# The order of a neighbourhood's 126 pixels on the partitions of an involution kernel: row by row instead of column by column

## The chip, the cores and the metric

The kernel runs on one core of a Trainium2 chip. The metric is the device time of that core in microseconds, from the start of the program to its end. One launch does the whole computation; the host only lays out weights.

## The reference, cut to what matters

The input is a batch of 8 images with 256 channels of 56 x 56 pixels in float32. Two blocks follow each other, each added to its own input.

```python
# block 0: an involution, whose 7 x 7 filter differs at every pixel, on the group-normalised input
ker = einsum('bchw,oc->bohw', gn(x), w_reduce) + b_reduce        # 256 -> 64 channels
ker = einsum('bchw,oc->bohw', ker, w_span) + b_span              # 64 -> 16 groups * 49 taps
patches = stack([xpad[:, :, i:i+56, j:j+56] for i in range(7) for j in range(7)])
x = x + (ker * patches).sum(taps)      # 16 channels of a group share a filter
# block 1: two 3 x 3 convolutions with ternary weights, batch norms over the whole batch, relus
out1 = relu(bn(conv(gn(x), tern(w1)))); out2 = bn(conv(out1, tern(w2)))
x = x + relu(out1 + out2)
```

The change touches block 0 alone.

## The kernel before, in words

**Stages.** The involution takes the first 1330 us of the program, image after image. The two convolutions follow, some 430 us of matmuls each, and then a last pass that combines and writes the output. The weights of the convolutions are quantized in the first 190 us.

**How the involution becomes matmuls.** Output pixels are worked on in tiles of PY x PX = 3 x 8. All that such a tile needs lies in a neighbourhood of QY x QX = 9 x 14 = 126 pixels (NQ). These 126 pixels are put on the partitions, which are the contracted dimension of a matmul. One operand is `q`: 126 neighbourhood pixels by 7 tiles (TX, one band across the image) by 128 columns, which are 64 channels in the upper and in the lower half of the image. The other is `a`: for each tile and group, a matrix from 126 neighbourhood pixels to 24 output pixels that holds the filter taps at the right places and zeros elsewhere. `apply_row` (from line 648) multiplies them: 56 small matmuls (line 662) for a band of tiles, whose result is evicted by ScalarE (line 670) and VectorE (line 671) and added to the image by GpSimd (line 674). There are 10 bands (TY), 4 channel quarters (NCQ) and 8 images: 320 bands in all.

**Where `a` comes from.** `generate` (from line 606) multiplies a slice of the stationary `wl` with the reduced features `kr` (line 626), and adds the span bias `bt` while evicting (lines 632 and 638). `wl` is a line of weights with zeros around it. The slice of 126 columns that starts at an offset depending on the output pixel (py, px) puts every tap on the partition of the neighbourhood pixel it belongs to. So the order of the neighbourhood pixels on the partitions enters in three places: in the slice's offset, in the layout of `wl` and `bt` that the host makes, and in the load of `q`.

**Where `q` comes from.** `prep` (from line 538) normalises a quarter of the next image, transposes it on TensorE and stores it with DMAs (line 547) to a scratch tensor in HBM, `xtd`. That tensor has 14 planes, one for each column j of a neighbourhood. A plane holds 36 rows (HQ) of 8 tile places (KX) of 128 floats. Neighbouring planes lie 147,456 B apart, neighbouring rows in a plane 4,096 B. One row of a band, 7 tiles by 128 floats, is contiguous: 3,584 B. `load_q` (line 591) fetches a band with one DMA of 126 such pieces, one for each partition, 441 KB. Before the change the outer dimension of its source is the 14 planes and the inner one 9 rows.

**What sets the order.** The program is written out in one order. In the loop over quarters (line 741) each band runs `apply_row`, then `prefetch`, which issues the load of a later band, up to five in advance (NQB = 5 buffers), then one or two queued transfers (`tasks`: loads of the next image on line 449, stores of finished quarters on line 688, stores to `xtd`), then a tenth of the next quarter's `generate`, then statistics on VectorE. A load's buffer comes free when the matmuls five bands earlier are done. All of these DMAs are issued by SyncE, one after the other. Loads of the next image's pixels are handed out during quarter 0, their statistics run on VectorE in quarter 1, and `prep` runs in quarters 2 and 3. The loads of an image's first bands can be issued only when its stores to `xtd` have been, which happens at the end of quarter 3 (lines 773 to 775).

Of the kernel before, what the change touches and what calls it, by code (L numbers as in the profile page):

```python
# [15 lines left out]
P = 128  # L16
# [3 lines left out]
K, PAD, G = 7, 3, 16  # L20
# [7 lines left out]
NCQ = C // CH  # L28
GQ = G // NCQ
# [4 lines left out]
PY, PX = 3, 8  # L34
TY, TX = 10, W // PX
# [2 lines left out]
NE = 2 * TX  # L38
QY, QX = PY + K - 1, PX + K - 1
NQ = QY * QX  # L40
LEAD = (PX - 1) * QY + PY - 1
WL = LEAD + NQ

KX = TX + 1
HQ = TY * PY + K - 1
EX = HQ * KX
# [26 lines left out]
def involution_tri_block_kernel(  # L75
# [356 lines left out]
    with ExitStack() as ph1:  # L432
# [3 lines left out]
        def ps_tile(name):  # L436
            return ps_p.tile([P, 2, 512], F32, tag="ps", name=name)
# [72 lines left out]
        def reduce(b, py):  # L510

            n = len(range(py, HH, PY))
            for i0 in range(0, n, TY // 2):
                m = min(TY // 2, n - i0)
                ps = ps_tile(f"pk_{b}_{py}_{i0}")
                r0 = i0 * PY + py
                for c in range(NCQ):
                    for h in range(2):
                        rows = slice(h * CH, (h + 1) * CH)
                        src = xs[b, c].rearrange("p (r w) -> p r w", w=W)  # L520
                        nc.tensor.matmul(ps[:, h, :m * W], wrn[rows, c, :],  # L521
                                         src[rows, r0:r0 + (m - 1) * PY + 1:PY, :],
                                         start=(c == 0), stop=(c == NCQ - 1))
                src = ps[:, :, :m * W].rearrange("p h (k x) -> p h x k", x=PX)
                whole = min(m, TY - 1 - i0)
                nc.scalar.activation(
                    kr[py][:, :, :NT].rearrange("p x (h k) -> p h x k", h=2)
                    [:, :, :, i0 * TX:(i0 + whole) * TX],
                    src[:, :, :, :whole * TX], AF.Identity, bias=brn)
                if whole < m:  # L530
                    nc.scalar.activation(
                        kr[py][:, :, NT:].rearrange("p x (h k) -> p h x k", h=2),
                        src[:, :, :, whole * TX:], AF.Identity, bias=brn)
# [57 lines left out]
        def load_q(b, c, ty):  # L591

            q = qpool.tile([P, TX, P], F32, tag="q", name=f"q_{b}_{c}_{ty}")
            d = xt_d[b % 2][c][:]
            src = bass.AP(d.tensor, d.offset + PY * ty * KX * P,
                          [[EX * P, QX], [KX * P, QY], [1, TX * P]])
            nc.sync.dma_start(q[:NQ].rearrange("p k c -> p (k c)"), src)
            return q

        def views(a):  # L600

            n = NT * GQ * NP
            return (a[:NQ, :n].rearrange("q (t f) -> q t f", t=NT),
                    a[:NQ, n:].rearrange("q (t f) -> q t f", t=NE))

        def generate(b, c, a):

            whole, rest = (v.rearrange("q t (g p) -> q g p t", g=GQ) for v in views(a))  # L610
            for u in range(NU):
                gp, (p0, n) = u // len(UNITS), UNITS[u % len(UNITS)]
                ps = ps_tile(f"pg_{b}_{c}_{u}")
                on_act = u in ON_ACT
                nt = NT + (NE if p0 < PX else 0)
                for j in range(n):
                    py, px = (p0 + j) // PX, (p0 + j) % PX
                    o = LEAD - px * QY - py
                    for i in range(2):
                        rows = slice(i * CR, (i + 1) * CR)  # L620

                        if on_act:
                            dst = ps[:NQ, i, j * nt:(j + 1) * nt]
                        else:
                            dst = ps[:NQ, i, j:n * nt:n]
                        nc.tensor.matmul(dst, wl[rows, c, gp, o:o + NQ], kr[py][rows, px, :],  # L626
                                         start=True, stop=True)
                g0 = 2 * gp
                if on_act:
                    for i in range(2):  # L630
                        for j in range(n):
                            nc.scalar.activation(  # L632
                                whole[:, g0 + i, p0 + j], ps[:NQ, i, j * nt:(j + 1) * nt],
                                AF.Identity, bias=bt[:, c, g0 + i, p0 + j:p0 + j + 1])
                else:
                    for dst, t0, t1 in ((whole, 0, NT), (rest, NT, nt)):
                        if t0 < t1:
                            nc.vector.tensor_tensor(  # L638
                                dst[:, g0:g0 + 2, p0:p0 + n].rearrange("q g p t -> q g t p"),
                                ps[:NQ, :, t0 * n:t1 * n].rearrange("q i (t p) -> q i t p", p=n),  # L640
                                bt[:, c, g0:g0 + 2, p0:p0 + n].unsqueeze(2).to_broadcast(
                                    [NQ, 2, t1 - t0, n]),
                                ALU.add)
                if c == NCQ - 1 and b + 1 < B and gp == GP - 1 and p0 + n in (PX, 2 * PX, NP):
                    reduce(b + 1, (p0 + n) // PX - 1)
                yield
# [33 lines left out]
        def prefetch(b):  # L680
            while queue and queue[0][0] <= b and len(loads) < NQB:
                k = queue.pop(0)
                loads[k] = load_q(*k)
# [45 lines left out]
        with tc.tile_pool(name="qp", bufs=1) as qp:  # L729
            quantize(wq_d[0], w1, qp, ps_flat, "w1")  # L730
            for _ in generate(0, 0, a_next):
                pass
            quantize(wq_d[1], w2, qp, ps_flat, "w2")
# [7 lines left out]
        for m, (b, c) in enumerate(quarters):  # L741
            a = a_next
            gen = iter(())
            if m + 1 < len(quarters):
                a_next = matrices(m + 1)
                gen = generate(*quarters[m + 1], a_next)
# [132 lines left out]
```

## Time and profile before

The time is 2488.15 us, the median of 3 runs (2482.87 to 2488.16). The profiled execution has a span of 2489.0 us.

| What | Share or size |
|---|---|
| TensorE matmuls busy, whole span | 1801.8 us, 72% |
| VectorE busy, whole span | 1659.4 us, 67% |
| ScalarE, GpSimd busy | 1093.8 us and 288.1 us |
| mean traffic, whole span | 198 GB/s, 493.14 MB |
| SyncE's DMA queue | 447.66 MB, 56.8% of the 16 DMA engines' span |
| loads of `q` | 320 DMAs of 441.0 KB |
| stores to `xtd` | 64 of 448, 128 of 168, 64 of 48 and 128 of 18 KB |
| loads of x, stores of x1 | 64 of 392 KB each |

The busy shares are averages over three stages with different limits. In the convolutions TensorE and VectorE are at 90% and more, in the last pass the DMA engines are. For the involution one has to read the slices between 190 and 1325 us alone, in which no compute engine is full.

### The profile page before, as it was taken

What the parts mean: (1) busy time and instruction counts of PE and PEld (TensorE: products, weight loads), DVE (VectorE), ACT (ScalarE), POOL (GpSimd) and SP (SyncE); (2) the same over time, 40 slices, a digit from 0 to 9 for tenths busy, and PEclk for the clock granted to TensorE, in tenths of its full rate; (3) what the DMA queues carried; (4) which work ended last, traced back from release to release, by engine and by line L of the source; (5) the groups of instructions that cost most, each with busy time, mean ns of one, the idle gap of its engine ahead of it and who ended that gap; (6) DMA issues with size and microseconds to landing.
All of it is one profiled execution on the core that took longest, in us unless ns stands there. A gap on an engine that the chain in (4) does not pass through costs nothing.

```text
span 2489.0 us, 68494 instructions
## 1 busy us (share of the span) xinstructions
PE 1801.8 (72%) x30120; PEld 1688.3 (68%) x30120; DVE 1659.4 (67%) x2458; ACT 1093.8 (44%) x2020; POOL 288.1 (12%) x427
## 2 busy tenths in 40 slices
PE   1416877878787787878775999999599999990000
PEld 1416766767676776767665999999599999990000
DVE  5465456464565645555556999999599999974444
ACT  0202333424243333433334567667356767754443
POOL 0101212213131221312211000000000000000000
PEclk9658998989898888989986999999799999995555
DMA  8536787878788877886765233232423323319998
GB/s 221 162 133 205 196 232 204 249 201 235 208 218 232 202 217 191 230 225 196 233 185 209 106 120 145 106 130 107 173 89 132 132 106 123 141 71 424 429 428 379
DMA packets 216197, 493.14 MB, mean 198 GB/s; under 512 B 38446, under 2 KB 139180, under 8 KB 207196
## 3 DMA queue, kind: packets, MB, share of 16 engines
q1 hardware_dynamic: 209584, 447.66, 56.8%
q10 hardware_dynamic: 6316, 41.09, 4.1%
q8 instruction: 238, 3.90, 0.7%
q14 instruction: 59, 0.48, 0.1%
HBM read 315.88 MB, written 172.81 MB: 196 GB/s over the span
## 4 chain that ended last, share of the span: by engine, by line
PE 62%; DMA 17%; DVE 10%; issue 6%; ACT 3%; SPq 1%; POOL 1%; ACTq 0%; DVEq 0%; POOLq 0%
PE c L385 34%; PE pg L626 13%; PE pa L662 8%; DMA y1f<-y1d 4%; PE pk L521 4%; DMA x<-in_x 3%; DVE a L638 3%; DMA out_y<-x1f 3%; PE pt L559 2%; ACT a L632 2%; DVE st L136 1%; DMA q<-xtd 1%; DMA w_w<-in_w 1%; DVE x1f L819 1%; DMA x1f<-x1d 1%
## 5 line engine op out<-in xcount | busy, mean ns | idle before, releaser
L385 PE MATMUL c<-pl,wq 128*128 128x392 f32 x4608 | 857.4, 348 | 52.1 <-ACT pl L291 32.2
L385 PEld LDWEIGHTS c<-pl,wq 128*128 128x128 f32 x4608 | 855.4, 189 | 53.8 <-ACT pl L291 33.0
L626 PE MATMUL pg<-kr,wl 64*126 64x140 f32 (+1 forms) x6144 | 508.0, 311 | 143.2 <-DVE a L638 63.3
L626 PEld LDWEIGHTS pg<-kr,wl 64*126 64x126 f32 x6144 | 434.9, 210 | 175.9 <-issue 128.6
L638 DVE TENSOR_TENSOR a<-pg,bt 126x84 f32<-126x84 f32 (+4 forms) x544 | 383.2, 740 | 76.5 <-PE pg L626 63.2
L662 PE MATMUL pa<-a,q 126*32 126x48 f32 x17920 | 298.9, 217 | 142.2 <-issue 96.6
L662 PEld LDWEIGHTS pa<-a,q 126*32 126x32 f32 x17920 | 246.5, 119 | 196.1 <-issue 130.2
L671 DVE SCALAR_TENSOR_TENSOR inv<-pa,half_sb,inv 128x168 f32<-128x168 f32 x320 | 120.2, 376 | 362.9 <-ACT inv L670 360.5
L670 ACT ACTIVATE inv<-pa,half_sb 128x168 f32<-128x168 f32 x320 | 127.4, 400 | 496.0 <-PE pa L662 480.9
L632 ACT ACTIVATE a<-pg,bt 126x126 f32<-126x126 f32 x768 | 218.4, 484 | 193.3 <-PE pg L626 193.1
L674 POOL TENSOR_TENSOR x<-x,inv 128x168 f32<-128x168 f32 x320 | 165.2, 516 | 811.0 <-DVE inv L671 755.2
L291 ACT CAST pl<-r 128x812 fp32r<-128x812 f32 x192 | 162.5, 867 | 148.7 <-DVE r L286 135.6
L136 DVE BATCH_NORM_STATS2 st<-x 128x6 f32<-128x392 f32 x256 | 138.1, 561 | 112.6 <-DMA x<-in_x 72.2
L348 ACT ACTIVATE dummy<-y,nc 128x1568 f32<-128x1568 f32 x128 | 205.4, 1605 | 15.6 <-DVE y L371 14.3
L292 DVE TENSOR_TENSOR pl<-r,pl 128x812 fp32r<-128x812 f32 x192 | 186.5, 998 | 32.1 <-ACT pl L291 31.2
L552 POOL TENSOR_SCALAR xn<-x,gn 128x784 f32<-128x784 f32 x64 | 108.7, 1698 | 127.2 <-PE pt L559 114.6
L800 ACT ACTIVATE xp<-raw,bi_bn,sc_bn 128x392 f32<-128x392 f32 (+1 forms) x128 | 84.8, 720 | 71.5 <-DVE a L286 57.1
L790 ACT ACTIVATE xp<-raw,gn 128x392 f32<-128x392 f32 (+1 forms) x128 | 85.2, 722 | 57.4 <-DVE a L286 50.7
L563 ACT COPY stg<-pt 112x1024 f32<-112x1024 f32 x64 | 67.2, 1051 | 89.0 <-DMA xtd<-stg 52.1
L272 POOL MEMSET xp<- 128x116 f32 x32 | 6.3, 196 | 820.2 <-DVE a L286 820.1
L817 DVE SCALAR_TENSOR_TENSOR y1f<-y2f,sc_bn,y1f 128x3136 f32<-128x3136 f32 x16 | 55.8, 3485 | 64.1 <-DMA y2f<-y2d 64.1
L819 DVE TENSOR_TENSOR x1f<-x1f,y1f 128x3136 f32<-128x3136 f32 x16 | 54.8, 3425 | 60.5 <-DMA out_y<-x1f 36.1
(127 smaller groups left out, 1397.1 us busy)
## 6 DMA issues: line engine op xcount, KB each, us to landing
q<-xtd SPq DMA_DIRECT2D x320, 441.0 KB
xtd<-stg SPq DMA_DIRECT2D x64, 448.0 KB
raw<-x1d SPq DMA_DIRECT2D x32, 812.0 KB
raw<-y1d SPq DMA_DIRECT2D x32, 812.0 KB
x<-in_x SPq DMA_DIRECT2D x64, 392.0 KB
x1d<-x SPq DMA_DIRECT2D x64, 392.0 KB
y1d<-y SPq DMA_DIRECT2D x32, 784.0 KB
y2d<-y SPq DMA_DIRECT2D x32, 784.0 KB
```

What stands on the lines that cost most here:

```text
L136: nc.vector.bn_stats(st[:, j, :], xt[:, j * NC:(j + 1) * NC])
L291: nc.scalar.copy(hi, r)
L292: nc.vector.tensor_tensor(lo, r, hi.bitcast(F32), ALU.subtract)
L348: nc.scalar.activation(dummy, y[:, to], f, bias=shift[:, to:to + 1], accum_out=stats[:, to, j, n:n + 1])
L385: nc.tensor.matmul(ps[:, to, :NM], wq[:, k, t, dx, to * P:(to + 1) * P], part[:, t, :, dx:dx + W], start=(c == 0), stop=(c == last))
L626: nc.tensor.matmul(dst, wl[rows, c, gp, o:o + NQ], kr[py][rows, px, :], start=True, stop=True)
L632: nc.scalar.activation(whole[:, g0 + i, p0 + j], ps[:NQ, i, j * nt:(j + 1) * nt], AF.Identity, bias=bt[:, c, g0 + i, p0 + j:p0 + j + 1])
L638: nc.vector.tensor_tensor(dst[:, g0:g0 + 2, p0:p0 + n].rearrange("q g p t -> q g t p"), ps[:NQ, :, t0 * n:t1 * n].rearrange("q i (t p) -> ...
L662: nc.tensor.matmul(ps[o:o + 32, k * 2 * n:(k + 1) * 2 * n], q[:NQ, k, o:o + 32], av[:, t + k, g * 2 * n:(g + 1) * 2 * n], start=True, stop ...
L670: nc.scalar.activation(iv, even, AF.Copy, scale=half_sb[:, 0:1])
L671: nc.vector.scalar_tensor_tensor(iv, odd, half_sb[:, 1:2], iv, ALU.mult, ALU.add)
L674: nc.gpsimd.tensor_tensor(xv, xv, iv.rearrange("p t (y x) -> p y t x", x=PX), ALU.add)
```

## The change

The neighbourhood pixels are put on the partitions row by row: pixel (row r, column j) goes to partition 14 r + j instead of 9 j + r. The source of a load then has the 9 rows as its outer dimension and the 14 planes as its inner one. The purpose that its author gives is that a load goes to nine DMA engines. The bytes, the pieces of 3,584 B and the number of DMAs are the same. The slice's offset in `generate` and the host's layout of `wl` and `bt` follow. `wl` gets shorter, since LEAD falls from 65 to 37 and the line from 191 to 163 columns.

```diff
-LEAD = (PX - 1) * QY + PY - 1
+LEAD = (PY - 1) * QX + PX - 1
 WL = LEAD + NQ
...
             src = bass.AP(d.tensor, d.offset + PY * ty * KX * P,
-                          [[EX * P, QX], [KX * P, QY], [1, TX * P]])
+                          [[KX * P, QY], [EX * P, QX], [1, TX * P]])
...
-                    o = LEAD - px * QY - py
+                    o = LEAD - py * QX - px
...
-    b_tile = np.zeros((QX, QY, NCQ, GQ, PY, PX), np.float32)
-    for kx in range(K):
-        o = LEAD + kx * QY
-        w_line[..., o:o + K] = ws[..., kx]
-        for ky in range(K):
+    b_tile = np.zeros((QY, QX, NCQ, GQ, PY, PX), np.float32)
+    for ky in range(K):
+        o = LEAD + ky * QX
+        w_line[..., o:o + K] = ws[..., ky, :]
+        for kx in range(K):
             for py in range(PY):
                 for px in range(PX):
-                    b_tile[px + kx, py + ky, :, :, py, px] = bs[:, :, ky, kx]
+                    b_tile[py + ky, px + kx, :, :, py, px] = bs[:, :, ky, kx]
```

## The prediction

> **What bounds the kernel now.** The edit lies in the involution, so I first cut it out of the span. The chain of waits, in order of time, puts the last apply matmul at about 1322 us; what follows is 2489 - 1322 = 1167 us that no edited line touches. Next I read the busy time by stretches. The columns are the stretch, its length, busy us of TensorE, weight loads, VectorE, ScalarE and GpSimd, the granted clock, the mean busy share of the 16 DMA engines, and GB/s.
>
> ```profile
> 540.90:541.70 0.80, 0.80 (x28) 0.68 (x22) 0.80 (x2) 0.21 (x1) 0.00 (x0) 0.50 0.87 349
> 484.50:514.50 30.00, 23.00 (x751) 20.32 (x751) 16.57 (x34) 10.47 (x34) 4.87 (x9) 0.95 0.91 260
> 514.50:547.80 33.30, 26.32 (x756) 23.40 (x754) 21.63 (x44) 10.06 (x34) 5.16 (x10) 0.79 0.68 183
> 547.80:591.90 44.10, 39.38 (x901) 34.17 (x900) 25.21 (x58) 17.69 (x45) 13.88 (x16) 0.92 0.82 223
> 591.90:625.10 33.20, 26.72 (x788) 23.27 (x786) 15.47 (x30) 14.53 (x39) 10.28 (x13) 0.95 0.89 250
> 280.00:1260.00 980.00, 778.87 (x21403) 687.89 (x21390) 525.85 (x1071) 354.71 (x1020) 227.29 (x321) 0.90 0.79 217
> ```
>
> Rows two to five are quarters 0 to 3 of one image. TensorE is busy 77, 79, 89 and 80% of them, the DMA engines 91, 68, 82 and 89%. So in quarters 0 and 3 the mean over 16 DMA engines is as high as any compute engine. The first row is a moment in which one band load runs alone: a share of 0.87 is 14 of 16 engines, and 349 / 14 = 24.9 GB/s each, or 144 ns for a 3,584 B piece. The load uses 14 engines[...].
>
> Then I asked who waits: first the list of waits (engine, line, releaser: us in total, times, longest), then the chain in order of time (start, us), around the start of the image at 480 us.
>
> ```profile
> SPq L597 <- PE pa L662: 389.2, 173, 8.5
> DVE st L136 <- DMA x<-in_x: 72.2, 23, 6.5
> PE pa L662 <- DMA q<-xtd: 11.7, 9, 2.6
> ```
> ```profile
> 480.93 5.71 DMA q<-xtd
> ...
> 505.19 9.25 DMA x<-in_x
> ```
>
> SyncE mostly waits for the matmuls that free a buffer, so loads normally run ahead. TensorE waits for a load only 9 times. Matching each load's issue with its semaphore's updates in the trace gives a median of 5.9 us from issue to landing; from landing to the first matmul that uses it there is a median of 9.0 us to spare. About one band in twenty has under 0.3 us to spare: nearly all of those are the first two or three of an image, whose loads wait for the stores to xtd, and the last few of the stage. VectorE waits 72.2 us for image loads, which are on the chain too.
>
> [...]image loads and stores touch 64 partitions, and their 6,272 B packets took a median of 412 ns here, 239 ns at best.
>
> **The change part by part.** On TensorE, VectorE, GpSimd and SyncE the built program has the same instructions in the same order, so the new offset and the layouts of bt and xtd cost nothing: shapes and operands' sizes are equal. The load of wl falls from 764 to 644 KB, once, beside the quantizing: nothing. The issue of a load (792 ns median on SyncE) still names 126 pieces; I take it as equal, and SyncE has idle time. The stores to xtd are untouched.
>
> What is left is the load. Each of its engines carries 126 / 9 = 14 pieces instead of 126 / 14 = 9. A lone load becomes 5 x 0.144 = 0.72 us longer (4.4 us from issue to landing for the one at 538.4 us). Against a spare 9 us that is hidden. [...] I work it out per quarter from the packet records between the same bounds. Packets of 3,584 B started in quarters 0 to 3: 1590, 1229, 1382, 841. Other packets (6,272, 512 and 256 B), time over 16 engines: 7.6, 6.8, 17.3 and 19.1 us per engine.
>
> Lower bound, each piece at 144 ns: pieces / 9 x 0.144 = 25.4, 19.7, 22.1, 13.5 us. With the others: 33.0, 26.4, 39.4 and 32.6 us, in quarters of 30.0, 33.3, 44.1 and 33.2 us. Only quarter 0 is over, by 3.0. In the next image (quarters of 35.4, 34.1, 43.7, 33.7 us) none is. So 1.5 us per image.
>
> Upper value, today's engine time plus the added pieces: 3,584 B packets took 302.7, 245.4, 285.8 and 157.4 us summed over engines (191 ns each in quarter 0[...]), over 14 engines 21.6, 17.5, 20.4 and 11.2. Added are pieces x (1/9 - 1/14) x 0.144 = 9.1, 7.0, 7.9, 4.8. With the others: 38.3, 31.3, 45.6, 35.1 us, which is over by 8.3, 0, 1.5 and 1.9, or 11.7 us; the next image, in the same way, 4.5, 0, 2.1 and 0.8, or 7.4. Mean 9.6 us per image.
>
> I take the upper value. Part of the 191 ns is latency that a full queue hides, which speaks for less; but an engine that is fed in bursts from a window of five loads can't reach 100%, which speaks for more, and I let these cancel. Seven images have this traffic: 7 x 9.6 = 67 us. Image 7 has no next image to load and store; there, at image 0's start and at the stage's end, only bands without spare time count: three queued loads, 3 x 0.72 = 2.2 us each place, 7 us. For the other images' starts this lies inside quarter 0's excess. Sum 67 + 7 = 74 us: 2488 + 74 = 2562 us.
>
> Where it appears: a late q holds the matmuls of line 662; behind them in TensorE's order stand those of line 626, whose evictions feed the next quarter's matrices. Late image loads hold VectorE at line 136, with the evictions of line 638 queued behind it.
>
> **The rivals.** *The window hides it.* Idle stretches of quarters 1 and 2 (68 and 82% busy) take up the surplus, pieces run at 144 ns. Then 1.5 us x 7, plus 2.2 us at eight image starts and 3 at the end: 10 + 18 + 3 = 31 us, 2519 us. For it: 9 us to spare in the middle. Against: quarter 0 begins with none, and only five loads may be ahead.
>
> *Every piece keeps today's mean.* Over 280 to 1260 us 3,584 B packets took 6,828 us in sum. Over 9 engines that is 759 us, with 336 us of others 1095 us in 980, 12% over. On some 1080 us of stage that is 127 us, 2615 us[...]. For it: today's mean over the stretch is 202 ns.[...] Against: half the packets are at the floor, and added pieces follow others in a stream.
>
> *It turns faster.* If long packets come from 14 writers[...], nine meet less often, and image loads find seven engines empty. Were a third of VectorE's 72 us saved, with the loads hidden, it would be 2488 - 24 = 2464 us.[...]
>
> **How the numbers follow.** Nine engines bound the stage: 0.60, at 2562. Hidden mostly: 0.21. Mean kept: 0.10. Faster: 0.06. No change within 0.3% (7 us): 0.03. Below 2500 lie the last two and a little of the hidden case; above 2640 the further half of the mean-kept case: together under 0.2. So 2500 to 2640. Slower by over 0.3%: 0.60 + 0.21 + 0.10 = 0.91.
>
> **What would show it.** A load alone: a share of 0.56 and 224 GB/s. The mean share falls (seven engines idle more) while waits of line 662 for q rise from 11.7 us to over 50; quarter 0 grows most, quarter 1 least; 1167 us after the stage stay. I am wrong if q is landed in time in mid-image (slack of some 5 us or more) in quarters 0 and 3, or if pieces in a stream are not at 144 ns.

## The result, and the profile after

The changed kernel takes 2519.9 us (median of 4 runs, 2514.53 to 2530.69) against 2488.15 us before (2482.87 to 2488.7). The ratio is 1.0138, with a 95% interval of 1.0098 to 1.0178: 34 us slower, between 24 and 44 (the medians differ by 32). The forecast was 2562 us, so the direction was right and the loss less than half as large. The profiled run is the longest of the four (2530.69 us), so its stage shows 41 us of loss, not 34.

Two things in the description of the kernel need mending. `LEAD` falls to 35, not 37, and the line of weights to 161 columns, not 163 (its load is 644 KB in the trace). And the built program doesn't issue the image loads where the loop hands them out. In the trace, five of the eight halves of a next image are loaded as soon as a buffer is free, in the image before the one where the loop names them. Only the last three go out in quarter 0.

First the stretches of quarters 0 to 3 of the same image as in the prediction, then the whole stage (same columns as there):

```profile
490.30:523.20 32.90, 24.61 (x750) 21.62 (x750) 16.04 (x32) 10.30 (x34) 4.87 (x9) 0.90 0.71 219
523.20:562.20 39.00, 25.65 (x757) 22.90 (x756) 21.44 (x44) 10.08 (x34) 5.22 (x11) 0.82 0.58 175
562.20:607.80 45.60, 40.20 (x899) 35.19 (x898) 25.25 (x58) 17.82 (x45) 13.81 (x16) 0.89 0.74 215
607.80:644.30 36.50, 26.61 (x788) 23.33 (x787) 17.04 (x32) 14.58 (x39) 10.33 (x13) 0.90 0.80 227
280.00:1300.00 1020.00, 778.38 (x21329) 686.29 (x21330) 521.45 (x1068) 352.74 (x1015) 227.68 (x320) 0.89 0.70 208
```

The work of the engines is unchanged, the stretches are longer, and the mean DMA share fell from 0.79 to 0.70 while the nine engines that carry the loads got fuller (an estimate from the packet records, with the other traffic taken as spread evenly over 16: 98% of this stretch, where those of 14 filled 85% before). Quarter 1 grew most, from 33.3 to 39.0 us. Over images 0 to 6, from the first load of weights of each quarter's line 662 to the next, the quarters went from 233.7, 228.7, 319.1 and 236.5 us to 232.2, 255.5, 322.6 and 249.6. So quarter 1 has 27 us of the loss and quarter 3 has 13; quarter 0 has none. Such shares are to be read with care: in the control with two DMAs (below), which is as quick as the kernel before, quarter 1 is 11 us longer and quarter 2 is 14 us shorter. From the last apply matmul (1362 us) to the end there are 1166 us, as before (1167).

The list of waits; the first line is of the kernel before, which the prediction doesn't show:

```profile
ACT stg L563 <- DMA xtd<-stg: 52.1, 17, 5.6
```
```profile
SPq L597 <- PE pa L662: 388.6, 188, 9.4
DVE st L136 <- DMA x<-in_x: 134.6, 26, 9.9
ACT stg L563 <- DMA xtd<-stg: 80.3, 26, 6.7
PE pa L662 <- DMA q<-xtd: 28.7, 14, 5.1
```

TensorE's waits for a band load rose by 17 us (from 11.7), ScalarE's for the stores to xtd by 28 us (from 52.1), VectorE's for image loads by 62 us (from 72.2). The chain in order of time has two image loads near the start of this image's quarter 1:

```profile
514.70 11.68 DMA x<-in_x
526.47 1.97 DVE st L136 x4
...
539.19 10.65 DMA x<-in_x
549.86 1.98 DVE st L136 x4
```

Each load's issue, matched with its semaphore's updates, says the same: from issue to landing a band load takes a median of 7.5 us (5.9 before) and an image load 9.9 us (7.9). The median spare time from landing to use fell from 9.0 to 7.1 us, and in quarter 0 of images 1 to 6 from 6.6 to 2.3 us.

The number of engines can be counted. All packets, before and after:

```profile
DMA packets 216197, 493.14 MB, mean 198 GB/s; under 512 B 38446, under 2 KB 139180, under 8 KB 207196
```
```profile
DMA packets 214597, 493.01 MB, mean 195 GB/s; under 512 B 36846, under 2 KB 137580, under 8 KB 205596
```

1,600 packets under 512 B are gone, five for each of the 320 loads, and of the larger ones none. In the loads alone (below) there are 3,137 such packets for 224 loads column by column and 1,738 for 193 row by row, 14 and 9 a load. The 14 are as many as the engines that the share of 0.87 tells, so now there are 9. The trace doesn't record which they are, nor which pieces an engine gets.

### The profile page after: what moved, and what is told of

Its sections match the earlier page's. It is cut to its first block, busy times and chain, and to the rows that moved or that the text cites. A ratio compares the mean times of both kernels' runs of the same rounds, so it can differ in the third digit from the quotient of the medians.

```text
span 2528.9 us, 68494 instructions
## 1 busy us (share of the span) xinstructions
PE 1801.3 (71%) x30120; PEld 1686.3 (67%) x30120; DVE 1656.8 (66%) x2458; ACT 1092.9 (43%) x2020; POOL 288.8 (11%) x427
## 4 chain that ended last, share of the span: by engine, by line
PE 58%; DMA 23%; DVE 10%; issue 5%; ACT 2%; POOL 1%; SPq 1%; ACTq 0%; DVEq 0%; POOLq 0%
PE c L385 34%; PE pg L626 11%; PE pa L662 8%; DMA x<-in_x 6%; DMA q<-xtd 4%; DMA y1f<-y1d 4%; PE pk L521 3%; DVE a L638 3%; DMA out_y<-x1f 3%; PE pt L559 2%; DMA xtd<-stg 2%; DVE st L136 2%; DMA w_w<-in_w 1%; ACT a L632 1%; DVE x1f L819 1%
## 5 line engine op out<-in xcount | busy, mean ns | idle before, releaser
L626 PE MATMUL pg<-kr,wl 64*126 64x140 f32 (+1 forms) x6144 | 501.4, 308 | 126.0 <-DVE a L638 77.1
L626 PEld LDWEIGHTS pg<-kr,wl 64*126 64x126 f32 x6144 | 428.9, 207 | 158.9 <-issue 98.5
L136 DVE BATCH_NORM_STATS2 st<-x 128x6 f32<-128x392 f32 x256 | 138.2, 561 | 175.0 <-DMA x<-in_x 134.6
L348 ACT ACTIVATE dummy<-y,nc 128x1568 f32<-128x1568 f32 x128 | 205.4, 1605 | 15.6 <-DVE y L371 14.3
L563 ACT COPY stg<-pt 112x1024 f32<-112x1024 f32 x64 | 67.0, 1047 | 106.7 <-DMA xtd<-stg 80.3
L559 PE MATMUL pt<-ident_sb,xn 128*112 128x128 f32 x512 | 82.3, 313 | 35.4 <-ACT stg L563 17.2
```

The source lines that it names most:

```text
L136: nc.vector.bn_stats(st[:, j, :], xt[:, j * NC:(j + 1) * NC])
L348: nc.scalar.activation(dummy, y[:, to], f, bias=shift[:, to:to + 1], accum_out=stats[:, to, j, n:n + 1])
L559: nc.tensor.transpose(pt[:NSP, j * P:(j + 1) * P], xn[:, j].rearrange("p r k -> p (r k)"), ident_sb)
```

## The experiments

Theory A says that the engines which carry the loads have more work than time. Theory B says that the cost is the latency of image loads queued behind longer band loads, felt by VectorE. Theory C says that the row order has a cost of its own, such as the 147,456 B from one piece to the next in its source, where it was 4,096 B. Each ratio is against runs of the kernel before that were made beside it, so medians of different experiments are not to be subtracted.

### Statistics that don't wait for the late image loads

```diff
-                    image_stats(st, xs[b, c], j)
+                    image_stats(st, xs[b, c % 2 if b else c], j)
```

> Column by column (14 engines), but the statistics of the next image's quarters 2 and 3 are taken from its quarters 0 and 1, which land much earlier. The same number and size of instructions, but those statistics are of the wrong pixels. It takes away what makes VectorE wait for late image loads (55.8 us of waits between 200 and 1260 us). Theory A[...]: this kernel loses nothing much, 2470 to 2488 us. Theory B (the change's cost is the latency of image loads behind longer band loads, felt by VectorE): part of the 55.8 us is on the path here too, so 2440 to 2465 us.

> Row by row (9 engines), with the same statistics taken from quarters 0 and 1. Waits of VectorE for image loads were 118.1 us in the stage with this order. Theory A: [...]this stays at least 25 us above its column-by-column twin, at 2500 us or more. Theory B: the gap between the twins shrinks to 10 us or less, and this lands near 2455 to 2475 us, below the unchanged kernel before.

Measured: column by column 0.9986 of the kernel before (0.9963 to 1.0008), row by row 1.0078 (1.0049 to 1.0107). The gap between the twins is 0.9%, or 23 us, against 34 us: more than the 10 us of theory B and a little less than the 25 us of theory A. Waits for image loads, by the trace of each, column by column first:

```profile
DVE st L136 <- DMA x<-in_x: 37.0, 13, 6.3
```
```profile
DVE st L136 <- DMA x<-in_x: 78.7, 15, 9.4
ACT stg L563 <- DMA xtd<-stg: 75.3, 24, 6.1
PE pa L662 <- DMA q<-xtd: 32.0, 16, 4.6
```

Row by row, 56 us of VectorE's waits went and perhaps 15 us of time with them (1.0138 to 1.0078, but the intervals overlap). Column by column 35 us of waits went and the time stayed. Theory B fails as the whole cause: most of the gap is left, and with it the other two waits, which are as long as in the changed kernel (75.3 us after 80.3, 32.0 after 28.7).

### Shorter pieces

```diff
-                          [[KX * P, QY], [EX * P, QX], [1, TX * P]])
-            nc.sync.dma_start(q[:NQ].rearrange("p k c -> p (k c)"), src)
+                          [[KX * P, QY], [EX * P, QX], [1, 4 * P]])
+            nc.sync.dma_start(q[:NQ, :4].rearrange("p k c -> p (k c)"), src)
...
-                                         q[:NQ, k, o:o + 32],
+                                         q[:NQ, k % 4, o:o + 32],
```

> Row by row (9 engines), but each piece of a band load carries 4 of 7 tiles (2,048 B instead of 3,584 B); the matmuls of tiles 4 to 6 use tiles 0 to 2 again, so part of the result is wrong. Pieces, engines and instructions are the same; an engine of the nine carries 28.7 KB a band instead of 50.2 KB, less than the 32.3 KB of 14 engines before. Theories A and B[...]: the loss goes, 2450 to 2490 us. Theory C (the order itself costs, by the 147,456 B steps between pieces or by the number of engines a load is handed to): 10 us or more of the loss stay, 2500 us or more.

> Column by column with pieces of 4 of 7 tiles, as in after_q4 (matmuls of tiles 4 to 6 use tiles 0 to 2 again, so part of the result is wrong). With 9 engines that gave 2390 us. If the loss is only bytes on the busiest engines, neither order fills an engine here and the two are within 8 us: 2382 to 2398 us. If the order costs by itself (theory C), this one is 15 us or more faster: 2375 us or less.

Measured: row by row 2390.25 us, 0.9631 (0.9604 to 0.9657); column by column 2368.52 us, 0.9512 (0.9467 to 0.9557). The row order came out below every range that a theory had given it. With all instructions of the compute engines left in, a load of 4/7 of the bytes saves 92 and 121 us, so the loads' bytes cost time in both orders, also on 14 engines. But the saving isn't bytes alone. The same columns as above, column order first:

```profile
280.00:1200.00 920.00, 766.23 (x22866) 675.07 (x22862) 551.64 (x1126) 367.52 (x1068) 237.60 (x342) 0.95 0.67 179
280.00:1200.00 920.00, 763.95 (x21963) 674.80 (x21960) 535.37 (x1096) 359.67 (x1046) 231.29 (x329) 0.93 0.65 176
```

The granted clock was 0.95 and 0.93 here, against 0.90 in the prediction's last row. From the first apply matmul to the last, TensorE is busy 838 and 853 us, against 890 us before. So up to 52 and 38 us of the savings are the same matmuls done faster; whether the clock rose because the waits went isn't shown. The change itself doesn't have this rival: its TensorE is busy 891 us, at 0.89.

The pair still differs by 1.2% (30 us; 28 us by the medians, each against its own runs of the kernel before), where I expected under 8 us. By the expectation's own words that spoke for theory C, until the loads were measured alone (below).

### Fewer engines in the column order

```diff
-            src = bass.AP(d.tensor, d.offset + PY * ty * KX * P,
-                          [[EX * P, QX], [KX * P, QY], [1, TX * P]])
-            nc.sync.dma_start(q[:NQ].rearrange("p k c -> p (k c)"), src)
+            m = NQ // 2
+            for g in range(2):
+                src = bass.AP(d.tensor, d.offset + (g * QX // 2 * EX + PY * ty * KX) * P,
+                              [[EX * P, QX // 2], [KX * P, QY], [1, TX * P]])
+                nc.sync.dma_start(
+                    q[g * m:(g + 1) * m].rearrange("p k c -> p (k c)"), src)
```

> Column by column, each band load cut into two DMAs of 7 planes, which go to 7 engines each: 18 pieces an engine and band instead of 9 (before) or 14 (row by row). Theory A: [...]the stage grows by 13% or more: 2620 us and more. Theory B: only latency grows, twice as far as from 14 to 9 engines: 2550 to 2590 us. Theory C (order, not engines): as before but for SyncE's added issues, 2480 to 2500 us.

The control cuts the load in two as well, but along the piece, so that both DMAs keep the 14 planes (`[1, 4 * P]` and `[1, 3 * P]` in place of `[1, TX * P]`). The DMA of 4 tiles is that of the short pieces alone (below): 254 GB/s at 118 ns for 2,048 B are 14.6 records at once, as whole pieces on 14 engines have 14.3 (261 GB/s at 197 ns). That the DMA of 3 tiles has 14 engines too was not shown:

> Control for col7: column by column, each band load cut into two DMAs that both go to 14 engines (4 tiles and 3 tiles of each piece). It doubles SyncE's issues of loads without moving bytes to fewer engines. If col7's 113 us are the 7 engines' doing, this stays near the kernel before: 2480 to 2510 us. If the doubled issue is to blame: 2570 us or more.

Measured: on 7 engines 2598.89 us, 1.0465 (1.0441 to 1.0490), or 116 us slower; the control 2486.39 us, 0.9981 (0.9964 to 0.9998). So neither the second issue nor shorter pieces cost, and the number of engines does, in the old order too. Theory C can't explain this one. The loss lies between the 62 to 102 us of theory B and the 132 us or more of theory A, so neither theory's sum was right. On 7 engines TensorE waits for the loads themselves:

```profile
PE pa L665 <- DMA q<-xtd: 128.5, 64, 6.0
```

The control's trace holds a warning about reading waits:

```profile
DVE st L136 <- DMA x<-in_x: 118.8, 27, 6.9
PE pa L665 <- DMA q<-xtd: 25.9, 14, 4.0
```

These are nearly the waits of the row-by-row kernel (134.6 and 28.7 us), in a kernel that is as quick as the one before. The waits for stores to xtd were 50.5 us there, not 80.3.

### Band loads alone

A kernel with nothing but the 320 loads, five in flight, after zeros are written to xtd and the output. Everything else of the computation is left out. The two orders differ in the source's dimensions, as in the change. Each of these kernels ran once, so their times have no interval.

> Nothing but the 320 band loads, column by column, five in flight, after zeros are written to xtd and to the output; no matmuls, no other traffic in the stretch read. It measures what a load costs 14 engines by itself. If the long pieces of the kernel before (mean 202 ns at 144 ns undisturbed) come from 14 engines being at work at once, the mean stays near 180 ns or more here and a load takes 1.6 us (275 GB/s). If they come from the other traffic or from gaps between bursts, it falls to about 145 ns and a load takes 1.3 us (345 GB/s).

> The same, row by row: 14 pieces on each of 9 engines. If fewer engines at once shorten the pieces: about 145 to 150 ns each, 2.0 to 2.1 us a load (215 to 224 GB/s), so 0.4 to 0.5 us more than column by column, not 0.72. If not: the piece costs the same as in the column-by-column run, and a load 14/9 of its time. If the 147,456 B steps slow the reads (theory C): pieces over 160 ns and a load over 2.2 us.

> Band loads alone, each as two DMAs on 7 engines (18 pieces an engine and band). At 144 ns a piece, as on 9 engines: 2.6 us a band, 0.87 us over the 14 engines' 1.72. One cause (the kernel loses in proportion to the load alone; 34 us for 0.26 us is 130 us per us): 0.8 to 0.95 us over, which fits col7's 113 us. If a load alone is under 2.3 us or over 2.9 us, the proportion fails.

> Band loads alone, column by column, pieces of 4 of 7 tiles (2,048 B). At the 263 GB/s of loads_col: 0.98 us a load. One cause: before_q4's gain of 121 us at 130 to 165 us per us asks for 0.75 to 0.95 us less than 1.72, so 0.77 to 0.97 us.

> The same, row by row on 9 engines. At 25 GB/s an engine: 14 x 82 ns = 1.15 us a load. One cause: it is 0.15 to 0.25 us over its column-by-column twin, since the whole kernels differ by 1.2% (some 30 us). Theory C (the row order has a cost of its own): the two loads alone differ by less than 0.1 us.

SyncE's timeline (start us, us, engine, line, instruction, tiles, count) gives the time in which the loads are issued, for column order, row order, 7 engines, and short pieces in column and in row order:

```profile
124.58 562.98 SPq L148 DMA_DIRECT2D q<-xtd  x320
```
```profile
122.56 643.94 SPq L148 DMA_DIRECT2D q<-xtd  x320
```
```profile
123.44 823.67 SPq L150 DMA_DIRECT2D q<-xtd  x640
```
```profile
123.19 334.93 SPq L148 DMA_DIRECT2D q<-xtd  x320
```
```profile
128.92 385.38 SPq L148 DMA_DIRECT2D q<-xtd  x320
```

Over 320 bands these are 1.76, 2.01, 2.57, 1.05 and 1.20 us a band. One stretch each of column order, row order and 7 engines (stretch, length, GpSimd, clock, DMA share, GB/s):

```profile
400.00:600.00 200.00, 0.00 (x0) 1.00 0.90 274
```
```profile
400.00:600.00 200.00, 0.00 (x0) 1.00 0.58 229
```
```profile
400.00:600.00 200.00, 0.00 (x0) 1.00 0.45 179
```

The shares are 14.4, 9.3 and 7.2 of 16 engines. 9 and 7 engines are each as quick as the lone load in the prediction (24.9 GB/s): 229 / 9 = 25.4 and 179 / 7 = 25.6 GB/s. 14 engines at once are not: 274 / 14 = 19.6 GB/s. The packet records agree: once the queue was full a piece took a mean of 144 ns on 9 and on 7 engines and 197 ns on 14. The mean piece came as expected in both orders. The difference of the loads didn't: 0.25 us, where I expected 0.4 to 0.5. So taking the load from 14 to 9 engines costs 14 x 144 - 9 x 197 = 243 ns, not 5 x 144 = 720. Nothing points to the window of five loads as what holds 14 engines back: their piece records fill the time as closely (9 x 197 = 1.77 us in 1.73 us a load) as those of 9 engines (14 x 144 = 2.02 us in 1.97).

The 197 ns are a mean, though, over a rate that moved within the one run, while the program did the same all along. Early and late stretch of column order:

```profile
200.00:300.00 100.00, 0.00 (x0) 1.00 0.91 239
500.00:600.00 100.00, 0.00 (x0) 1.00 0.90 288
```

That is 217 ns a piece and then 179, or 1.89 and 1.57 us a load, so the 0.25 us could be 0.08 or 0.40. On 9 and on 7 engines the rate hardly moved (226 to 230 and 179 GB/s). What moves it isn't known, nor at which rate the whole kernel's loads run.

Now set each whole kernel beside its load alone, both against column order with whole pieces (ratio less 1, times 2488 us):

| Kernel | Load alone | Whole kernel | us for one us of load |
|---|---|---|---|
| row by row | +0.25 us | +34 us | 137 |
| 7 engines | +0.81 us | +116 us | 143 |
| short pieces, row by row | -0.56 us | -92 us | 164 |
| short pieces, column by column | -0.71 us | -121 us | 171 |

About 140 for losses and 164 to 171 for gains: one proportion covers all four roughly. The 7 engines came as it asked. Short pieces in column order did not: it asked for 0.77 to 0.97 us a load, and 1.05 came, and the gains hold the faster matmuls too. The two kernels with short pieces differ by 0.15 us alone, which at these rates is 21 to 26 us of the 30 found, inside the uncertainty of the two ratios. Theory C isn't needed for it, and on 9 engines the piece stays at 144 ns with 147,456 B from one to the next.

### What makes pieces long on 14 engines

> Only band loads on 14 engines, as loads_col (196 ns a piece, 1.72 us a load), but each load reads 126 pieces 4,096 B apart, so the engines read within half a MB and not from planes 147,456 B apart; the partitions written are the same, the data are not. If where 14 engines read at once makes the pieces long: pieces fall to 145 to 165 ns and a load to 1.3 to 1.5 us. If it is the writing side, or any 14 engines at once: it stays at 185 to 200 ns and 1.7 us.

> As loads_col, with one unused row of 4,096 B behind each plane of xtd: the planes lie 151,552 B apart instead of 147,456. If this plane distance is what makes 14 engines collide in reading: pieces of 145 to 170 ns, a load of 1.3 to 1.5 us. If not: 196 ns and 1.72 us as in loads_col.

> The kernel before, column by column on 14 engines, with the planes of xtd 151,552 B apart; nothing left out. If the plane distance makes pieces long, a load gets cheaper by up to 0.4 us on each of 14 engines and the stage, which bytes bound (pieces of 4 tiles gave 120 us), gets 20 to 60 us shorter: 2425 to 2465 us. If it doesn't matter: within 8 us of the kernel before.

The edits are `[[KX * P, NQ], [1, TX * P]]` for the source in the first, and one constant in the other two:

```diff
-EX = HQ * KX
+EX = (HQ + 1) * KX
```

Measured alone: pieces 4,096 B apart took 521.18 us for 320 loads, 1.63 us each at a mean piece of 181 ns, between the two ranges expected; padded planes 574.70 us, 1.80 us each at 203 ns. The padded whole kernel: 1.0005 (0.9986 to 1.0025), no change. So padding gives nothing. Reading from far apart can't be the whole reason, since pieces 4,096 B apart are far above 144 ns too. Whether it is a part isn't settled, because this kernel's rate moved as well:

```profile
200.00:300.00 100.00, 0.00 (x0) 1.00 0.90 293
500.00:600.00 100.00, 0.00 (x0) 1.00 0.91 276
```

Early it is well above column order's 239 GB/s, late below its 288. What limits 14 engines at once to 240 to 290 GB/s in these loads stays open; the writing side wasn't tried apart. No version that computes everything was found clearly quicker than the kernel before; the nearest is the control with two DMAs on 14 engines, 0.9981.

## Why the prediction was right or wrong, point by point

**Right: the direction, and the path in outline.** The number of engines is 9, which nothing in the trace of the kernel before shows (packets under 512 B now, a share of 0.58 with 229 GB/s alone). The share of all 16 fell from 0.79 to 0.70 and the waits for q rose, though to 28.7 us and not to over 50. The edits costed at nothing cost nothing: what follows the stage kept its length (1166 us after 1167). On 9 engines alone a piece takes 144 ns, as in the lone load, with 147,456 B from one piece to the next in the source. Of the signs of being wrong that the prediction names, one came in part: in quarter 3 a band of images 1 to 6 still landed a median of 8.7 us ahead of its use.

**Wrong: the term "pieces x (1/9 - 1/14) x 0.144".** It adds five pieces at 144 ns to nine whose long duration it keeps. Alone, under a full queue, the load got 14 x 144 - 9 x 197 = 0.24 us longer and not 0.72, because the nine got shorter as well. The prediction had both numbers, 144 ns for a lone load and 191 to 202 ns in the stage; that the difference goes with the number of engines it listed under "it turns faster" and gave no part in the main sum. The reason that was to cancel this, that engines fed from a window of five loads can't reach 100%, fell too: alone, five in flight kept 9 engines full (0.58 x 16 = 9.3). How much shorter the pieces got in the whole kernel its trace tells less clearly. Their mean fell from 202 to 174 ns, by which a load's records on one engine still grew by 14 x 174 - 9 x 202 = 0.62 us. But these records hold waiting: before, over half of the pieces took under 145 ns, and the longest ninth a mean of 519. In the lone load of the prediction it is the first 14 pieces that are long, 325 to 1,115 ns, and the later ones are mostly at 140.

**Wrong: counting only what goes beyond a quarter's length.** With 0.24 us in place of 0.72 the prediction's own sum gives 2.3 us for the image shown and nothing for the next, some 10 us in all; with 0.40 us, the most that the load alone allows, some 20. Both are less than the 24 to 44 us measured. So a term that was too large and a threshold that was too strict made up for each other in part. The runs show a loss that goes about with the load's own time instead of such a threshold: 137 to 143 us over the 320 bands for each us that a load alone gets longer, on 9 engines (where the 0.25 us is as uncertain as said) and on 7. So a band loses some 0.44 of what its load gets longer; why it is this fraction isn't shown.

**Wrong: one sum for each quarter.** Quarter 0 was to grow most and quarter 1 least. It was the other way round. In the image shown, quarter 0 now starts 1448 pieces instead of 1590 and quarter 1 1395 instead of 1229: the surplus was handed on to the next quarter, where the loop has its waits for image loads. Over images 0 to 6 it is the same, 10,478 for 11,128 and 9,361 for 8,628. The records of 9 engines in quarter 0 (15.6 us over 16 engines of band pieces and 7.4 of image packets, taken as spread evenly) add up to 15.6 x 16 / 9 + 7.4 = 35.1 us in a stretch of 32.9. So packet records overlap, as they do alone, where 14 engines fill 0.90 of 16 and 14/16 is 0.875. Their sum is no measure of what an engine can hold; a load's time under a full queue is a better one.

**The rival "the window hides it" gave 2519 us, which is what came, and for reasons that hold only in part, so the agreement is in part luck.** Its 144 ns a piece is what 9 engines take alone, and quarter 1 did take up quarter 0's surplus. But its largest term, 18 us at the images' starts, wasn't found: quarter 0 didn't grow, and bands used within 0.35 us of landing went from 17 to 19. What it left out, VectorE behind image loads, is perhaps 11 to 15 us by the experiment with early statistics.

**The other rivals.** "Every piece keeps today's mean" fell: 174 ns over 280 to 1300 us instead of 202. "It turns faster" was right that pieces are shorter on fewer engines (why isn't shown) and wrong on the sum: 14 x 144 is still more than 9 x 197. Two of the prediction's readings are a little off without effect: the shortest packet of 6,272 B took 236 ns, not 239, and the other traffic from 280 to 1260 us comes to 328 us, not 336.

## What to carry to other kernels

In this case a transfer's price on fewer DMA engines couldn't be had from today's packet times plus the extra packets: measure the load alone on both numbers of engines under a full queue, long enough to see whether its rate moves, and compare its whole time. Here the sum said 0.72 us a load and the loads alone 0.25. Where transfers run as close to full as here, a wait in the list shows where the lateness came out, not what it costs; take the wait away before believing its microseconds. In the control VectorE waited 118.8 us for image loads, against 72.2 before, at 0.9981 of the time. And a stage with loads far ahead of their use (9 us to spare) can still lose time to their bytes: shortening the pieces told it in one run (121 us). Look at the granted clock there (0.95 against 0.90) before putting all of the gain down to bytes.

## What the runs showed of the hardware that was not expected

14 DMA engines together took a mean of 197 ns for a 3,584 B piece where 9 or 7 took 144, so five more engines raised the rate from 229 to 261 GB/s only (from the 41st load on), not by 14/9. With pieces of 2,048 B it was 118 and 87 ns, 254 and 221 GB/s. On 14 engines the rate moved within a run by itself, from 239 to 288 GB/s in column order; on 9 (226 to 230) and 7 (179) it hardly did. On 14 engines the pieces were far above 144 ns at each distance in HBM that was tried: means of 181 ns at 4,096 B, 197 at planes of 147,456 B and 203 at 151,552 B, in single runs whose rates moved.
